# A macaron layer on one core: the first block's start, the weight counts and the last stores rearranged

## The chip, the cores and the metric

The kernel runs on one core of a Trainium2 chip. A core has a matrix engine (TensorE, PE in the profile; its weight loads are PEld), a vector engine (VectorE, DVE), an engine for activation functions (ScalarE, ACT), a general one (GpSimd, POOL) and SyncE (SP), which here only starts transfers. Each works through its own instructions in order; they meet at semaphores. Transfers between the chip's memory (DRAM) and the on-chip memory are queued by SP, ACT or POOL and carried out by 16 shared DMA engines. PE writes into eight banks of a separate accumulation memory (PSUM).

The metric is the device time of one launch in microseconds (us). Three timed runs of the kernel before gave 1446.25 in the median (1444.95 to 1446.85).

## The reference, cut to what matters

```python
x = L0_attn_x                                         # (4, 1024, 256), float32
x = x + 0.5 * ffn(layernorm(x))
x = x + s4d(layernorm(x))                             # long convolution by FFT, gelu, @ W.T + b
x = x + 0.5 * ffn(layernorm(x))                       # the same weights again

def ffn(x):                                           # D = 256, HID = 1024
    h = silu((x @ w1.T) * w1_s) * ((x @ w2.T) * w2_s)
    h = gelu((h @ h1.T) * h1_s)
    h = gelu((h @ h2.T) * h2_s)
    return (h @ w3.T) * w3_s                          # the weights hold -1, 0 and 1
```

## The kernel before

The 4096 rows are cut into eight blocks of 512. The blocks go through the first feed-forward turn (`f0` to `f7`) and, after the convolution of their batch entry, through the second (`g0` to `g7`): sixteen blocks, one after another, in the loop at L817 to L831.

**One block.** `norm` (L199) takes the mean and variance of each row on DVE (`bn_stats`, `bn_aggr`), the square root on ACT, then a reciprocal and four scalings on DVE. `transposed` (L220) turns the rows on PE into two banks `pt` and brings them back as `xt`: a copy rounded to the fast format fp32r and, by `low_part` (L216), what the rounding lost, so that two fast products stand for one exact one. `ffn` (L248) then runs layer one for m = 0 to 7 (banks `pa`, `pb`; silu on ACT, the gate product on DVE, L260, a rounded copy `ha` on ACT and its low part on DVE), layers two and three (banks `p`, gelu on ACT, copies `h`), and the output product `po` (L296), two row groups to a bank. The result is scaled on DVE (L304), the block's rows are added on POOL (L312) and SP stores it (L313). A block has 64 products 128x512 in layer one and 128 in each of the two others, and 64 products 128x256 for `po`.

**Beside it.** The generator `all_aside` makes the convolution's kernel, its spectrum, and for each batch entry the mixing `mix` (forward transform, product with the spectrum, inverse transform, output product), whose steps are called from inside the blocks: `tick` is called 15 times a block. `prepare` loads and normalises the next block ahead; `ahead` calls it. Last in `all_aside` come the weight counts (`weight_checks`, L315): the fp32r weights are exact for -1, 0 and 1, and 44 loads of 256 KB each bring the given weights again and count on DVE (L329) where the held ones differ. Two are handed out per tick. At the end the counts are summed, a product over partitions gives the flag `bad` (L838 to L842), every engine reads it, and if it is not zero the whole is computed again in plain fp32. With these inputs it is zero.

**What sets the order.** The program records instructions; a scheduler of the framework then places each engine's instructions by the readiness it expects of them. An instruction of a later block can so be placed ahead of one of an earlier block. Once placed, the order is fixed: an engine that waits holds up all that is behind it.

**The start.** SP issues, in this order: the first block's 512 KB (L170), the constants (L180, with the epsilon of the norm in a column), the scales, the second block, `k_in` (L188 and L189, the inputs of the convolution's kernel), the w3 scales, `wt` and `bias`, then blocks three and four. POOL issues w1 and w2, each in two halves by rows k (L183, L184), so that any product needs all columns' halves, then h1 and h2 in four parts each (L192) and w3 (L193).

Of the kernel before, what the change touches and what calls it, by code (L numbers as in the profile page):

```python
# [2 lines left out]

# [1 line left out]

# [12 lines left out]
P = 128  # L18
# [10 lines left out]
NA, NB = 64, 16  # L29
A0, A1 = 8, 8  # L30
JQ = J // 2
N_CHECKS = 44

EPS = 1e-5
# [14 lines left out]
C_A0, C_A1 = 0, A0  # L49
C_B = C_A1 + A1  # L50
C_RE = C_B + NB
C_IM, C_MINUS_RE, C_SGN, C_EPS, C_HALF_PI = range(C_RE + 1, C_RE + 6)
C_N = C_HALF_PI + 1
CST_WIDTH = 56

# [5 lines left out]
def shape_constants():  # L61

    p = np.arange(P)
    j = np.arange(J).reshape(2, JQ).T.reshape(-1)
    k = np.arange(P)
    pos = J * p[:, None, None] + j[None, :, None]
    angle = (2 * k[None, None, :] + 1) * pos % (4 * L) * (2.0 * np.pi / (4 * L))
    forward = np.stack([np.cos(angle), -np.sin(angle)], axis=2)  # L70

    inverse = forward.transpose(3, 1, 2, 0) * (2.0 / L)

    cst = np.zeros((P, C_N), np.float64)
    cst[:, C_A0 : C_A0 + A0] = NB * np.arange(A0)
    cst[:, C_A1 : C_A1 + A1] = NB * A0 * np.arange(A1)
    cst[:, C_B : C_B + NB] = np.arange(NB)
    real = (np.arange(P) // N2) % 2 == 0
    cst[:, C_RE] = real
    cst[:, C_IM] = ~real  # L80
    cst[:, C_MINUS_RE] = -1.0 * real
    cst[:, C_SGN] = np.where(real, 1.0, -1.0)
    cst[:, C_EPS] = EPS
    cst[:, C_HALF_PI] = HALF_PI
    return (
        np.ascontiguousarray(forward.astype(np.float32)),
        np.ascontiguousarray(inverse.astype(np.float32)),
        cst.astype(np.float32),
    )
# [3 lines left out]
def macaron_layers(  # L93
# [70 lines left out]
    def positions(t, b, j, n=2):  # L164
        return t[b].rearrange("(p j) d -> p j d", j=J)[:, j : j + n, :]

    def load_x(t, blk, name):
        b, g = divmod(blk, J // JT)
        xb = work.tile([P, JT, D], F32, tag="xb", name=name, bufs=3)
        nc.sync.dma_start(xb, positions(t, b, g * JT, JT))  # L170
        return xb

    def rows(w):
# [2 lines left out]

    weights_from = nc.gpsimd if split else nc.sync

    x_first = load_x(x, 0, "x_f0")
    nc.sync.dma_start(cst_sb[:, 0:C_N], cst)  # L180
    nc.sync.dma_start(sc_sb, scales)
    for k in range(DC):
        weights_from.dma_start(w1_sb[:, k, :], rows(w1)[:, k, :])  # L183
        weights_from.dma_start(w2_sb[:, k, :], rows(w2)[:, k, :])  # L184
    x_second = load_x(x, 1, "x_f1")
    k_in = half("k_in", 4, DD)
    k_in2 = half("k_in2", 4, DD)
    nc.sync.dma_start(k_in, kin[:, 0:4, :])  # L188
    nc.sync.dma_start(k_in2[:, 0, :], kin[:, 4, :])  # L189
    for t, src in ((h1_sb, h1), (h2_sb, h2)):  # L190
        for k in range(0, KH, 2):
            weights_from.dma_start(t[:, k : k + 2, :], rows(src)[:, k : k + 2, :])  # L192
# [3 lines left out]
    nc.sync.dma_start(bias_sb, bias.partition_broadcast(P))  # L196


    def norm(t, name):  # L199

        stats = small.tile([P, JT, 6], F32, tag="stats", name=f"stats_{name}")
        mv = small.tile([P, JT, 2], F32, tag="mv", name=f"mv_{name}")
        rstd = small.tile([P, JT], F32, tag="rstd", name=f"rstd_{name}")
        for i in range(JT):
            nc.vector.bn_stats(stats[:, i, :], t[:, i, :])
        for i in range(JT):
            nc.vector.bn_aggr(mv[:, i, :], stats[:, i, :])
        nc.scalar.activation(rstd, mv[:, :, 1], AF.Sqrt, bias=column(C_EPS))
        yield
        nc.vector.reciprocal(rstd, rstd)  # L210
        for i in range(JT):
            ts(t[:, i, :], t[:, i, :], mv[:, i, 0:1], rstd[:, i : i + 1], ALU.subtract, ALU.mult)
        yield


    def low_part(t, src):  # L216

        tt(t[:, 1, :], src, t[:, 0, :].bitcast(F32), ALU.subtract)  # L218

    def transposed(xn, name):  # L220

        xt = []
        for k in range(DC):
            pt = bank(f"pt_{name}_{k}")
            for i in range(JT):
                nc.tensor.transpose(  # L226
                    pt[:, i * P : (i + 1) * P], xn[:, i, k * P : (k + 1) * P], ident
                )
            t = ring(f"xt_{name}_{k}", parts, TB, dtype=wide)
            nc.vector.tensor_copy(t[:, 0, :], pt)  # L230
            if split:
                low_part(t, pt)
            xt.append(t)
        return xt

    def linear(ps, w, m, acts):
        n = len(acts)
# [7 lines left out]
                    stop=(k == n - 1 and part == parts - 1),  # L245
                )

    def ffn(xt, src, dst, blk, name, tick, ahead):  # L248

        ha = []
        for m in range(KH):
            pa, pb = bank(f"pa_{name}_{m}"), bank(f"pb_{name}_{m}")
            linear(pa, w1_sb, m, xt)
            linear(pb, w2_sb, m, xt)
            g = half(f"g_{name}_{m}")
            t = ring(f"ha_{name}_{m}", parts, TB, dtype=wide)
            nc.scalar.activation(g, pa, AF.Silu, scale=sc_sb[:, 0, m : m + 1])  # L259
            stt(g if split else t[:, 0, :], pb, sc_sb[:, 1, m : m + 1], g, ALU.mult, ALU.mult)  # L260
            if split:
                nc.scalar.copy(t[:, 0, :], g)  # L262
                low_part(t, g)
            ha.append(t)
        for layer, w in ((2, h1_sb), (3, h2_sb)):
            hb = []
            for m in range(KH):
                ps = bank(f"p{layer}_{name}_{m}")
                linear(ps, w, m, ha)
                t = ring(f"h{layer}_{name}_{m}", parts, TB, dtype=wide)  # L270
                g = half(f"g{layer}_{name}_{m}") if split else t[:, 0, :]
                nc.scalar.activation(g, ps, AF.Gelu, scale=sc_sb[:, layer, m : m + 1])  # L272
                if split:
                    nc.scalar.copy(t[:, 0, :], g)  # L274
                    low_part(t, g)
                hb.append(t)
                if layer == 3:
                    ahead()
                if m < KH - 1:
                    tick()  # L280
            ha = hb
        ahead(last=True)
        tick()
        b, g = divmod(blk, J // JT)
        rest = []
        for i in range(0, JT, 2):
            xr = half(f"xr_{name}_{i}", 2, D)
            nc.sync.dma_start(xr, positions(src, b, g * JT + i))
            rest.append(xr)
        for i in range(0, JT, 2):  # L290
            xr = rest[i // 2]
            ps = bank(f"po_{name}_{i}")
            for e in range(2):
                for k in range(KH):
                    for part in range(parts):
                        nc.tensor.matmul(  # L296
                            ps[:, e * D : (e + 1) * D],
                            ha[k][:, part, (i + e) * P : (i + e + 1) * P],
                            w3_sb[:, k, :],
                            start=(k == 0 and part == 0),  # L300
                            stop=(k == KH - 1 and part == parts - 1),
                        )
            y = half(f"y_{name}_{i}", 2, D)
            stt(  # L304
                y,
                ps.rearrange("p (e d) -> p e d", e=2),
                0.5,
                w3s_sb[:, None, :].to_broadcast([P, 2, D]),
                ALU.mult,
                ALU.mult,  # L310
            )
            nc.gpsimd.tensor_tensor(y, xr, y, ALU.add)  # L312
            nc.sync.dma_start(positions(dst, b, g * JT + i), y)  # L313

    def weight_checks():  # L315

# [9 lines left out]
        for n, (src, held) in enumerate(todo):  # L326
# [8 lines left out]
                ALU.not_equal,  # L335
                accum_out=miss[:, n : n + 1],
            )
            if n % 2:
                yield

# [457 lines left out]
    def all_aside():  # L800


        yield from kernel_steps()
        yield from kernel_spectrum()
        for b in range(B):
            while ("f", 2 * b + 1) not in done:
                yield
            yield from mix(b)
            done.append(("m", b))
        if split:  # L810
            yield from weight_checks()

    aside = all_aside()
    for _ in norm(x_first, "f0"):
        pass
    xt = transposed(x_first, "f0")
    for n, (turn, blk) in enumerate(blocks):  # L817
        following = []
        steps = [prepare(*b, following) for b in blocks[n + 1 : n + 2]]
# [5 lines left out]
                next(step, None)  # L825

        src, dst = (x, x1) if turn == "f" else (x2, out)
        ffn(xt, src, dst, blk, f"{turn}{blk}", lambda: next(aside, None), ahead)
        done.append((turn, blk))
        xt = following  # L830
    for _ in aside:  # L831
        pass


    if split:
        total = small.tile([P, 1], F32, name="total")
        ones = small.tile([P, 1], F32, name="ones")
        nc.vector.memset(ones, 1.0)  # L838
        nc.vector.tensor_reduce(total, miss[:, 0:N_CHECKS], axis=mybir.AxisListType.X, op=ALU.add)
        ps = psum.tile([1, 1], F32, tag="ps", name="p_bad")  # L840
        nc.tensor.matmul(ps, total, ones, start=True, stop=True)
        nc.vector.tensor_copy(bad, ps)  # L842


def macaron_kernel(tc: tile.TileContext, *args):
# [72 lines left out]
```

## Time and profile before

| What | us |
|---|---|
| median of three timed runs | 1446.25 |
| the profiled execution, its own time | 1447.1 |
| its span, first to last instruction | 1445.3 |
| TensorE matmul busy | 1418.6 |
| VectorE busy | 835.7 |
| ScalarE busy | 672.7 |
| GpSimd busy | 76.1 |
| statistics of the first block start | 4.54 |
| first product of layer one starts | 17.07 |
| layer two of the first block runs unbroken from | 40.29 |
| output product of the first block starts | 98.15 |
| last output product ends | 1437.67 |

A row of a group or timeline reads: start, duration, engine, line, operation, what it writes and from what, shapes, how many; in square brackets how long the engine stood idle before it and what ended that. A matmul's record overlaps the next one's: 128x512 products are recorded with 390 ns, but 256 of them in a row take 58.03 us, 0.227 us each. "clock" is the share of its full clock that PE was granted.

### The profile page before, as it was taken

To read this page: it belongs to the slowest core of one execution; us is meant where nothing else is said; L and a number is where in the kernel's file an instruction comes from. 1 tells how busy PE (TensorE), PEld (TensorE's weight loads), DVE (VectorE), ACT (ScalarE), POOL (GpSimd) and SP (SyncE) were. 2 spreads that over 40 slices of the span, in tenths; PEclk is the share of its full clock that TensorE was granted. 3 is DMA by queue.
4 is the path that set the end of the run, shared out by engine and by line. 5 is a ranking of instruction groups with operands and counts; after the bars stand their busy time and mean duration, and the time that the engine had idled before them with its cause. 6 is when DMAs were issued, how large, how long until landed. Compare 5 with 4: busy or idle time off the path is not lost.

```text
span 1445.3 us, 18115 instructions
## 1 busy us (share of the span) xinstructions
PE 1418.6 (98%) x7074; PEld 1199.6 (83%) x7074; DVE 835.7 (58%) x1580; ACT 672.7 (47%) x1026; POOL 76.1 (5%) x75
## 2 busy tenths in 40 slices
PE   5999999999999999999999999999999999999997
PEld 4788888888888888888888888888888888888886
DVE  5777666862745487542676622866447666564511
ACT  3677458743534454334553433534345343443432
POOL 2000000000000000020000010000010000100000
PEclk9999999999999999999999999999999999999999
DMA  9110000100122030130130130220121201633000
GB/s 363 40 37 8 15 31 0 45 1 30 44 74 73 30 102 16 44 109 8 31 106 15 55 102 1 73 73 30 44 88 44 74 30 44 219 117 103 23 8 17
DMA packets 43038, 85.50 MB, mean 59 GB/s; under 512 B 4800, under 2 KB 10048, under 8 KB 42944
## 3 DMA queue, kind: packets, MB, share of 16 engines
q1 hardware_dynamic: 39152, 72.73, 15.4%
q0 software_dynamic: 3792, 11.54, 2.3%
q8 instruction: 57, 0.93, 0.3%
q14 instruction: 37, 0.30, 0.1%
HBM read 69.05 MB, written 15.20 MB: 58 GB/s over the span
## 4 chain that ended last, share of the span: by engine, by line
PE 93%; DMA 3%; DVE 3%; ACT 1%; issue 0%; POOL 0%; SPq 0%; POOLq 0%; DVEq 0%
PE p_f L240 31%; PE p_g L240 30%; PE po_g L296 4%; PE po_f L296 4%; PE pa_g L240 4%; PE pb_g L240 4%; PE pa_f L240 4%; PE pb_f L240 4%; PE pi L737 2%; PE pf_m L567 2%; PE pw L757 2%; PE pk L498 1%; DMA x_f<-in_x_dram 1%; DMA k_in<-in_kin_dram 1%; DMA x_g<-x 1%; PE pt_f L226 1%
## 5 line engine op out<-in xcount | busy, mean ns | idle before, releaser
L240 PE MATMUL p_f<-ha_f,h_sb 128*128 128x512 f32 x1024 | 239.9, 393 | 1.8 <-ACT ha_f L262 0.9
L240 PE MATMUL p_f<-h_f,h_sb 128*128 128x512 f32 x1024 | 238.9, 392 | 0.0
L240 PE MATMUL p_g<-h_g,h_sb 128*128 128x512 f32 x1024 | 236.0, 390 | 0.0
L240 PE MATMUL p_g<-ha_g,h_sb 128*128 128x512 f32 x1024 | 235.0, 390 | 0.0
L240 PEld LDWEIGHTS p_f<-ha_f,h_sb 128*128 128x128 f32 x1024 | 192.7, 189 | 43.7 <-ACT ha_f L262 1.7
L240 PEld LDWEIGHTS p_g<-h_g,h_sb 128*128 128x128 f32 x1024 | 192.2, 188 | 39.8
L240 PEld LDWEIGHTS p_g<-ha_g,h_sb 128*128 128x128 f32 x1024 | 192.1, 188 | 39.7
L240 PEld LDWEIGHTS p_f<-h_f,h_sb 128*128 128x128 f32 x1024 | 191.5, 188 | 39.7
L272 ACT ACTIVATE g_g<-p_g,sc_sb 128x512 f32<-128x512 f32 x128 | 88.3, 690 | 273.7 <-PE p_g L240 273.6
L218 DVE TENSOR_TENSOR h_g<-g_g,h_g 128x512 fp32r<-128x512 f32 x128 | 88.5, 691 | 215.2 <-ACT h_g L274 215.2
L218 DVE TENSOR_TENSOR h_f<-g_f,h_f 128x512 fp32r<-128x512 f32 x128 | 88.2, 691 | 202.9 <-ACT h_f L274 202.6
L272 ACT ACTIVATE g_f<-p_f,sc_sb 128x512 f32<-128x512 f32 x128 | 88.0, 689 | 219.1 <-PE p_f L240 217.2
L274 ACT CAST h_g<-g_g 128x512 fp32r<-128x512 f32 x128 | 79.4, 620 | 4.0
L274 ACT CAST h_f<-g_f 128x512 fp32r<-128x512 f32 x128 | 78.9, 618 | 3.2
L259 ACT ACTIVATE g_g<-pa_g,sc_sb 128x512 f32<-128x512 f32 x64 | 43.7, 688 | 68.2 <-PE pa_g L240 64.9
L240 PE MATMUL pa_f<-xt_f,w_sb 128*128 128x512 f32 x256 | 70.3, 395 | 1.9 <-DVE xt_f L230 1.2
L240 PE MATMUL pb_f<-xt_f,w_sb 128*128 128x512 f32 x256 | 69.2, 391 | 0.0
L240 PE MATMUL pa_g<-xt_g,w_sb 128*128 128x512 f32 x256 | 68.6, 390 | 0.0
L240 PE MATMUL pb_g<-xt_g,w_sb 128*128 128x512 f32 x256 | 68.4, 389 | 0.0
L296 PE MATMUL po_g<-w_sb,h_g 128*128 128x256 f32 x512 | 65.7, 289 | 1.7 <-DVE h_g L218 1.7
L296 PEld LDWEIGHTS po_g<-w_sb,h_g 128*128 128x128 f32 x512 | 63.8, 196 | 2.5 <-DVE h_g L218 2.3
L260 DVE SCALAR_TENSOR_TENSOR g_g<-pb_g,sc_sb,g_g 128x512 f32<-128x512 f32 x64 | 47.6, 748 | 30.9 <-PE pb_g L240 25.2
(216 smaller groups left out, 1632.0 us busy)
## 6 DMA issues: line engine op xcount, KB each, us to landing
h_sb<-in_h_dram POOLq DMA_DIRECT2D x8, 1024.0 KB, 22.8
given<-in_h_dram SPq DMA_DIRECT2D x32, 256.0 KB, 5.1
kr<-k_hat SPq DMA_DIRECT2D x20, 256.0 KB, 2.6
ki<-k_hat SPq DMA_DIRECT2D x20, 256.0 KB, 2.8
x_f<-in_x_dram SPq DMA_DIRECT2D x8, 512.0 KB, 4.1
xr_f<-in_x_dram SPq DMA_DIRECT2D x16, 256.0 KB, 4.1
x<-y_f SPq DMA_DIRECT2D x16, 256.0 KB, 2.4
xm<-x SPq DMA_DIRECT2D x8, 512.0 KB, 4.5
```

The source lines that it names most:

```text
L218: tt(t[:, 1, :], src, t[:, 0, :].bitcast(F32), ALU.subtract)
L226: nc.tensor.transpose(pt[:, i * P : (i + 1) * P], xn[:, i, k * P : (k + 1) * P], ident)
L240: nc.tensor.matmul(ps, w[:, k, m * P : (m + 1) * P], acts[k][:, part, :], start=(k == 0 and part == 0), stop=(k == n - 1 and part == parts ...
L259: nc.scalar.activation(g, pa, AF.Silu, scale=sc_sb[:, 0, m : m + 1])
L260: stt(g if split else t[:, 0, :], pb, sc_sb[:, 1, m : m + 1], g, ALU.mult, ALU.mult)
L272: nc.scalar.activation(g, ps, AF.Gelu, scale=sc_sb[:, layer, m : m + 1])
L274: nc.scalar.copy(t[:, 0, :], g)
L296: nc.tensor.matmul(ps[:, e * D : (e + 1) * D], ha[k][:, part, (i + e) * P : (i + e + 1) * P], w3_sb[:, k, :], start=(k == 0 and part == 0) ...
L498: nc.tensor.matmul(pk[0:NA, at + i, :, :].rearrange("p h b -> p (h b)"), a[:, i].rearrange("p a b -> p (a b)"), qd[d1 // per_tile][:, at + ...
L567: nc.tensor.matmul(ps[e][:, part, :], m[:, e, part, :], rows_of(q + JQ * e), start=True, stop=True)
L737: nc.tensor.matmul(banks[dc][e][:, q * P : (q + 1) * P], vs[q + JQ * e][:, part, dc * P : (dc + 1) * P], m[:, e, part, :], start=(part == ...
L757: nc.tensor.matmul(ps[:, e * D : (e + 1) * D], yts[dc][j // JQ][:, (j % JQ + e) * P : (j % JQ + e + 1) * P], wt_sb[:, dc, :], start=(dc == 0),
```

## The change

It has five parts.

1. **First block ahead on VectorE.** The first block's rows are loaded in two halves, one by SP and one by ACT. Its norm is recorded in two parts. Its transposes go by row group, so that both banks fill together, and ACT makes one of the two rounded copies. `ffn` of the first block is recorded inside `tc.issue_after(last_split.ins)`, so that its instructions are placed behind the last low part of the first block's transposes. The epsilon is a small tile set on DVE, no column of the constants, and ACT takes one square root of it at once, which loads its table.
2. **Weights by columns.** w1 and w2 come as columns 0 to 255 of both, then columns 256 to 1023 of both. The second block and `k_in` go to POOL's queue, behind those four loads and ahead of h1.
3. **Identity products until rows arrive.** 14 products of the 128x128 identity with itself, into a bank that nobody reads, stand first on PE.
4. **Weight counts spread.** After the first four blocks one count is handed out on every third tick, from a generator of its own; the sum and the flag follow in it after the 44th.
5. **Last stores smaller.** In the last block the last two row groups have a bank each; each is scaled and added on DVE and stored by itself (128 KB), where before both were scaled together, added on POOL and stored as 256 KB.

```diff
@@ loads
-    x_first = load_x(x, 0, "x_f0")
+    x_first = work.tile([P, JT, D], F32, tag="xb", name="x_f0", bufs=3)
+    for i, queue in ((0, nc.sync), (2, nc.scalar)):
+        queue.dma_start(x_first[:, i : i + 2, :], positions(x, 0, i))
+    eps = small.tile([P, 1], F32, name="eps", bufs=1)
+    nc.vector.memset(eps, EPS)
+    unused = small.tile([P, 1], F32, name="unused", bufs=1)
+    nc.scalar.activation(unused, eps, AF.Sqrt)
...
-    for k in range(DC):
-        weights_from.dma_start(w1_sb[:, k, :], rows(w1)[:, k, :])
-        weights_from.dma_start(w2_sb[:, k, :], rows(w2)[:, k, :])
-    x_second = load_x(x, 1, "x_f1")
+    for cols in (slice(0, 256), slice(256, HID)):
+        weights_from.dma_start(w1_sb[:, :, cols], rows(w1)[:, :, cols])
+        weights_from.dma_start(w2_sb[:, :, cols], rows(w2)[:, :, cols])
+    x_second = load_x(x, 1, "x_f1", queue=weights_from)
...
-    nc.sync.dma_start(k_in, kin[:, 0:4, :])
-    nc.sync.dma_start(k_in2[:, 0, :], kin[:, 4, :])
+    weights_from.dma_start(k_in, kin[:, 0:4, :])
+    weights_from.dma_start(k_in2[:, 0, :], kin[:, 4, :])
@@ transposed
+        for k, i in sorted(order, key=lambda o: o[1]) if first else order:
+            nc.tensor.transpose(
+                pts[k][:, i * P : (i + 1) * P], xn[:, i, k * P : (k + 1) * P], ident
+            )
+        xt = [ring(f"xt_{name}_{k}", parts, TB, dtype=wide) for k in range(DC)]
+        if first:
+            last = nc.vector.tensor_copy(xt[0][:, 0, :], pts[0])
+            nc.scalar.copy(xt[1][:, 0, :], pts[1])
...
+            if split:
+                last = low_part(xt[k], pts[k])
+        return (xt, last) if first else xt
@@ ffn, the output
-            nc.gpsimd.tensor_tensor(y, xr, y, ALU.add)
-            nc.sync.dma_start(positions(dst, b, g * JT + i), y)
+            add_on.tensor_tensor(y, xr, y, ALU.add)
+            nc.sync.dma_start(positions(dst, b, g * JT + i, n), y)
+            if final and i + 2 == JT:
+                for e in range(2):
+                    ps = bank(f"po_{name}_{i + e}")
+                    result(ps, i + e, 1)
+                    finish(ps[:, 0:D], y[:, e : e + 1, :], rest[i // 2][:, e : e + 1, :],
+                           i + e, 1, nc.vector)
+            else:
+                ps = bank(f"po_{name}_{i}")
+                result(ps, i, 2)
+                finish(ps, y, rest[i // 2], i, 2, nc.gpsimd)
@@ weight_checks
-            if n % 2:
-                yield
+            yield
+        total = small.tile([P, 1], F32, name="total")
...
+        nc.vector.tensor_copy(bad, ps)
@@ the loop
+    def tick():
+        nonlocal ticks
+        next(aside, None)
+        ticks += 1
+        if ticks > 4 * STEPS and ticks % 3 == 0:
+            next(checks, None)
+    warm = bank("warm")
+    for i in range(N_WARM):
+        nc.tensor.matmul(warm[:, 0:P], ident, ident, start=(i == 0), stop=(i == N_WARM - 1))
-    for _ in norm(x_first, "f0"):
+    for _ in norm(x_first, "f0", parts_of=2):
         pass
-    xt = transposed(x_first, "f0")
+    xt, last_split = transposed(x_first, "f0", first=True)
...
-        ffn(xt, src, dst, blk, f"{turn}{blk}", lambda: next(aside, None), ahead)
+        with tc.issue_after(last_split.ins) if n == 0 else nullcontext():
+            ffn(xt, src, dst, blk, f"{turn}{blk}", tick, ahead, n + 1 == len(blocks))
```

`STEPS` is 15, `N_WARM` 14. The weights, the products and their number are the same, save the 14 of part 3.

## The prediction

> **What bounds the kernel now.** I read the page first, then busy time by stage, then the timeline of the first 45 us and of the end, and last the one block where TensorE waits in between. Times in us are from the start of the profiled execution.
>
> ```profile
> PE 1418.6 (98%) x7074; PEld 1199.6 (83%) x7074; DVE 835.7 (58%) x1580; ACT 672.7 (47%) x1026; POOL 76.1 (5%) x75
> ...
> PEclk9999999999999999999999999999999999999999
> ...
> PE 93%; DMA 3%; DVE 3%; ACT 1%; issue 0%; POOL 0%; SPq 0%; POOLq 0%; DVEq 0%
> ```
>
> TensorE (PE) is the bound and 93% of the chain that ended last. What can be saved lies where it does not run. The busy time by stage shows where:
>
> ```profile
> core 0: us, PE busy (x) PEld busy (x) DVE busy (x) ACT busy (x) POOL busy (x), PEclk, DMA share, GB/s
> 0.00:17.07 17.07, 2.26 (x9) 1.48 (x9) 6.66 (x28) 3.16 (x4) 8.62 (x18) 1.00 0.93 307
> 17.07:40.29 23.22, 20.65 (x77) 15.00 (x77) 16.87 (x42) 13.16 (x21) 0.88 (x1) 1.00 1.13 400
> 40.29:106.06 65.77, 65.77 (x317) 55.70 (x318) 47.18 (x106) 46.95 (x61) 1.60 (x1) 0.97 0.05 17
> 106.06:1268.43 1162.37, 1160.55 (x5849) 983.60 (x5847) 695.15 (x1273) 544.18 (x842) 57.25 (x49) 1.00 0.16 52
> 1437.67:1445.30 7.63, 0.10 (x2) 0.00 (x0) 0.74 (x2) 0.00 (x0) 1.26 (x1) 0.68 0.18 56
> ```
>
> Three places: the head (no product before 17.07, then 77 records in 23.2 us), a little before 1268.43, and 7.63 us after the last product. The head in order of time:
>
> ```profile
> 10.82 1.08 DVE L205 BATCH_NORM_STATS2 stats_f<-x_f 128x6 f32<-128x256 f32 x3 [4.60 <-DMA x_f<-in_x_dram]
> ...
> 12.90 0.34 DVE L414 TENSOR_SCALAR k_in<-k_in,cst_sb 128x128 f32<-128x128 f32 x1 [0.92 <-DMA k_in<-in_kin_dram]
> 13.10 1.38 DVE L212 TENSOR_SCALAR x_f<-x_f,mv_f,rstd_f 128x256 f32<-128x256 f32 x4
> ...
> 17.07 1.72 PE L240 MATMUL pa_f<-xt_f,w_sb 128*128 128x512 f32 x2 [1.20 <-DVE xt_f L230]
> ...
> 23.95 1.41 DVE L205 BATCH_NORM_STATS2 stats_f<-x_f 128x6 f32<-128x256 f32 x4 [4.50 <-DMA x_f<-in_x_dram]
> ...
> 26.50 1.40 DVE L205 BATCH_NORM_STATS2 stats_f<-x_f 128x6 f32<-128x256 f32 x4 [0.86 <-DMA x_f<-in_x_dram]
> ...
> 28.10 2.03 DVE L260 SCALAR_TENSOR_TENSOR g_f<-pb_f,sc_sb,g_f 128x512 f32<-128x512 f32 x3
> ```
>
> VectorE (DVE) works in order. The first block's scaling (13.10) stands behind the second block's statistics and behind `k_in`, though its own data was there at 4.54. Later the first gate product (28.10) stands behind the statistics of blocks three and four. So layer two runs without a break only from 40.29, where the chain of waits has 244 of its 256 products left; they end at 97.5.
>
> **The head, step by step.** *Until the first product.* The rows come in two halves on two queues, the same 512 KB, so I keep 4.4 for their landing. Then, on DVE without anything between: 4 statistics at 0.33 apart, 4 aggregates at 0.09, 2 reciprocals at 0.16, 4 scalings at 0.33 make 3.3; ScalarE's (ACT) square roots lie beside it, their table now loaded before; some 0.4 for handing over. Last scaling at 8.1, last transposes 8.6, copy 0.68: the first product could start at about 9.5 instead of 17.07. The constant moved to a memset and the dummy square root cost nothing: DVE and ACT are idle until 4.5.
>
> *The weights.* The built order of the changed program puts on PE, after pa and pb of m=0 and m=1 (four products), pa and pb of m=2. Those need columns 256 to 1023 of w1 and of w2, and PE does not pass by a waiting product. So the real start is W, the landing of the last of the four weight loads; the early columns save only five products. W comes from bytes:
>
> ```profile
> GB/s 0 62 372 141 251 337 354 364 361 392 397 386 388 395 382 397 400 397 409 411 408 408 422 419 422 430 419 411 430 408 422 419 401 393 378 122 5 15 0 0
> ```
>
> These are 40 slices of 1.125 us of the first 45 us; summed: 1.31 MB by 6.75, 2.52 by 10.1, 3.41 by 12.4, 4.28 by 14.6, 9.28 by 27.0. In the run before, GpSimd's (POOL) queue waits show the four loads landed at about 7.5, 10.4, 12.5 and 14.1, with 1.07, 1.61, 2.66 and 3.44 MB at or ahead of them: 1.5 to 2.8 after the sum reached it, 2.0 in the mean. In the changed program rows (0.52), small constants (0.04) and weights (2.10) go with what SyncE (SP) issues meanwhile: w3 scales, wt, bias (0.52), the third block (0.52), and, from 8.7 when the first buffer is free, the fourth (0.52). That is 3.97 to 4.23 MB: reached at 13.8 to 14.5, plus 2.0. **W = 16.2**; the ends are 13.3 (no SP load ahead: 3.2 MB, plus 1.5) and 17.3.
>
> Here a rule stands against the row. The Trainium skill (DMA: Bandwidth & Descriptors, "Anatomy of one DMA") prices a load at 2.0 us plus bytes over 436 GB/s; with 2.6 MB of rows and weights that would be some 8 us after issue at 1.3, W near 9.5, and a gain of 15. The trace has 14.1 for the same 2.1 MB of weights, because other queues share the engines; I take the row.
>
> *From W.* PE has 59 of layer one's 64 products left. The first ones before ran at 0.43 apart until 20.4 (3.4 us), then 0.227 (58.03/256). Will the 14 identity products change this? 128x128 fp32 products of this form take 0.11 (pi: 7.14/64) at full clock, twice that when slow: 3 us, from 2.5 to 5.5, before ten idle microseconds. The skill (TensorE: Matmul & The Clock Gate, Part 1) says that some 3.4 us of work opens the clock and an idle window of the same length closes it. By that they buy nothing, and by the trace's 3.4 us row they are too short as well; if they held, 8 x 0.2 = 1.6 would come off. I take nothing. Layer one: 8 x 0.43 + 51 x 0.227 = 15.0, if ACT and DVE keep up. They have 1.3 and 1.27 each per m against PE's 1.82, but DVE now waits for block two and `k_in`, which moved behind the weights on POOL's queue: 0.78 MB more, W+2.1. From there the order gives the first gate at W+4.1; ACT then carries two table loads (1.28 each) and a root, gates 2 to 4 at W+9.5 to W+10.7, the last low part at W+17.5. PE needs that one at W+18.2. So it just fits, by 0.7, and PE flows from layer one into two. The h1 weights (9.3 MB, 27.0 plus 2.0 = 29) come before W+17 = 33.
>
> End of layer three: W + 15.0 + 58.0 = 89.2 against 97.5. **Gain 8.3** (11.2 and 7.2 at the ends of W; the slow clock of 40 to 45, which cost 1.7, goes with the gap). Later blocks follow 8.3 earlier.
>
> **The weight counts.** Before, 44 loads and counts came in one stretch:
>
> ```profile
> 1268.43 6.79 PE L296 MATMUL po_g<-w_sb,h_g 128*128 128x256 f32 x42 [1.31 <-DVE h_g L218]
> ...
> 1270.00:1275.00 5.00, 5.00 (x32) 5.00 (x32) 2.08 (x6) 0.00 (x0) 1.28 (x1) 0.68 0.13 49
> ```
>
> DVE was full from 1250 to 1270, h7's low part came late, PE lost 1.31 + 0.41, and then ran at clock 0.68 for 5 us (1.6): 3.3 in all. Spread out, each count is 0.69 + 0.08 of DVE, five per block, 3.9 in some 81 to 102 us of a block where DVE is at most 78% busy: hidden. Each also adds a load to SP and holds a buffer; in the order a buffer comes free 4 to 20 DVE instructions (2.4 to 12 us) before the count, while a load takes 0.33 + 2.4 to 5.1. Some counts will hold DVE for 1 to 2 us. ACT's results wait on DVE then, but PE uses them a layer later, save at layer ends. SP's stores queue behind such a load too; their readers come a block later. Bounds: nothing, and 0.3 for each of 9 blocks; I take 0.5. **Gain 2.8.** The final sum and flag product (0.2) move inside; nothing.
>
> **The last stores.**
>
> ```profile
> 1437.69 0.69 DVE L304 SCALAR_TENSOR_TENSOR y_g<-po_g,w3s_sb 128x512 f32<-128x512 f32 x1 [2.78 <-PE po_g L296]
> 1438.52 1.26 POOL L312 TENSOR_TENSOR y_g<-xr_g,y_g 128x512 f32<-128x512 f32 x1 [2.18 <-DVE bad L842]
> ```
>
> From the last product to the store's issue: 0.69, then the flag's 0.13, POOL 1.26: 2.1. After: two DVE operations on 256 columns, 0.42 each (the 256-wide scaling has 0.41), 0.06 between: 0.9. The landing (3.3) and the 2.2 behind it stay; half the bytes may save 0.3 more, and PE's branch at the end (4.1 from 1439.1) starts earlier too. **Gain 1.2.**
>
> **The sum.** 8.3 + 2.8 + 1.2 = 12.3: span 1445.3 to 1433.0, profiled execution 1447.1 to 1434.8. The median of the timed runs is 0.85 under that one: 1446.25 - 12.3 = **1434.0 us**. A change of 0.2% (2.9 us) is about what can be told from none.
>
> **Rivals.**
> *The weights come sooner, or the clock stays open* (0.15). For it: only the SP loads stand between 13.3 and 16.2. Against it: they are issued by 5 us. W = 13.3 and the clock open: 11.2 + 1.6 + 2.8 + 1.2 = 16.8, 1429.5.
> *The first block still stands behind DVE* (0.17). For it: the margin is 0.7, and DVE again waits for block two first. If `k_in` lands 4 us later or ACT's table loads fall worse, layer two starts 4 later and the slow clock (1.7) returns: gain 6.6, 1439.6.
> *The counts cost more than they free* (0.05): slower. Mechanism: a count waits for its load on DVE just before a block's last low part, and PE stalls as it did at 1268 for 3.3. Head and tail and the freed stall give 12.8; four of nine blocks with it eat that, all nine give 1446.25 - 12.8 + 29.7 = 1463. Against it: in the trace some forty loads of k_hat factors reach DVE in the same way, and no wait for them is among its 25 longest.
> *The order is not what is said* (0.01): the built order shows the first block's DVE work unbroken, so hardly; 1446.
>
> **How the numbers follow.** 0.62 for 1434.0, with 1431 to 1437 of its own; the rest as above. The range reaches over most of the two neighbours: 1429.5 to 1439. Faster 0.93, same 0.02, slower 0.05.
>
> **What would show it.** First product at 9 to 10, four or five products, then a wait ended by w_sb until about 16; layer two unbroken from about 31, layer three's end near 89; no wait of PE for h_g of over 0.5 at a block's end; store issued 0.9 to 1.0 after the last product. Wrong would be a wait for ha_f in layer two over 2 us, or waits for counts that PE feels.

## The result and the profile after

The changed kernel took 1436.53 us in the median (1435.89 to 1437.07, four runs), the one before beside it 1445.62 (1444.95 to 1446.85, four runs): a ratio of 0.9936, 95% interval 0.9919 to 0.9953. That is 9.1 us less; the prediction had 12.3 less, 1434.0. The profiled execution has a span of 1435.2 against 1445.3, 10.1 less.

The page of the changed kernel, its busy row and its chain by engine:

```profile
PE 1420.1 (99%) x7102; PEld 1203.3 (84%) x7102; DVE 834.3 (58%) x1584; ACT 674.2 (47%) x1030; POOL 79.1 (6%) x77
...
PE 97%; DVE 1%; DMA 1%; POOL 0%; issue 0%; POOLq 0%
```

PE rose from 93% of the chain to 97%: what is left is almost all matrix work. Where the rest sits is in the busy time by stage (columns as in the prediction: PE, its weight loads, DVE, ACT, POOL, then clock, transfer share, GB/s):

```profile
10.45:16.75 6.30, 1.69 (x5) 0.86 (x5) 1.27 (x2) 1.25 (x1) 1.20 (x2) 0.91 1.09 413
16.75:22.60 5.85, 5.82 (x14) 4.66 (x15) 2.94 (x11) 1.42 (x3) 3.77 (x5) 0.52 1.13 424
22.60:33.08 10.48, 10.48 (x48) 8.65 (x47) 9.56 (x21) 9.32 (x15) 0.00 (x0) 1.00 1.13 419
33.08:91.10 58.02, 58.02 (x258) 47.99 (x258) 42.98 (x109) 45.03 (x61) 0.00 (x0) 1.00 0.14 45
1428.28:1435.20 6.92, 0.00 (x0) 0.00 (x0) 0.85 (x2) 0.00 (x0) 0.00 (x0) 0.78 0.19 64
```

Five products run before 16.75, then PE is full but at clock 0.52, then full at 1.00. Layers two and three take 58.02 without a break and end at 91.10. The timeline of PE shows what the first stretch waits for:

```profile
2.58 6.33 PE L880 MATMUL warm<-ident 128*128 128x128 f32 x28 [2.58 <-POOL ident masks.py:199]
8.72 1.06 PE L248 MATMUL pt_f<-ident,x_f 128*128 128x128 f32 x8
10.45 0.50 PE L267 MATMUL pa_f<-xt_f,w_sb 128*128 128x512 f32 x1 [0.67 <-DVE xt_f L254]
...
13.43 0.50 PE L267 MATMUL pa_f<-xt_f,w_sb 128*128 128x512 f32 x1 [1.79 <-DMA w_sb<-in_w_dram]
16.78 0.77 PE L267 MATMUL pb_f<-xt_f,w_sb 128*128 128x512 f32 x1 [2.85 <-DMA w_sb<-in_w_dram]
```

The 14 identity products fill PE until 8.9; the last scaling of the rows was done at 7.5:

```profile
6.66 0.84 DVE L227 TENSOR_SCALAR x_f<-x_f,mv_f,rstd_f 128x256 f32<-128x256 f32 x2
```

Four products follow, then the fifth and sixth, pa and pb of m=2, each wait for the late columns of w1 and w2. The first gain, up to the end of layer three, is 97.5 - 91.1 = 6.4. The output products of the next four blocks keep this lead of 6.4, so the head accounts for all of it up to where the counts begin. The last product ends at 1428.28 instead of 1437.67, 9.39 earlier, so the counts brought 3.0. The end:

```profile
1427.49 2.54 SPq L341 DMA_DIRECT2D out_dram<-y_g  x2
1427.74 0.52 PE L323 MATMUL po_g<-w_sb,h_g 128*128 128x256 f32 x3
...
1428.30 0.42 DVE L332 SCALAR_TENSOR_TENSOR y_g<-po_g,w3s_sb 128x256 f32<-128x256 f32 x1 [0.97 <-PE po_g L323]
1428.76 0.42 DVE L340 TENSOR_TENSOR y_g<-xr_g,y_g 128x256 f32<-128x256 f32 x1
```

Scaling and addition take 0.9 as priced, to 1429.18. SP's two stores are one group here; the first was issued for 2.07 us, so the last went out only at 1429.6. From the last product to the end are 6.92 against 7.63: 0.7.

### The profile page after: what moved, and what is told of

Read it like the earlier page. It is cut to its first block, busy times and chain, and to the rows that moved or that the text cites. A ratio compares the mean times of both kernels' runs of the same rounds, so it can differ in the third digit from the quotient of the medians.

```text
span 1435.2 us, 18151 instructions
## 1 busy us (share of the span) xinstructions
PE 1420.1 (99%) x7102; PEld 1203.3 (84%) x7102; DVE 834.3 (58%) x1584; ACT 674.2 (47%) x1030; POOL 79.1 (6%) x77
## 4 chain that ended last, share of the span: by engine, by line
PE 97%; DVE 1%; DMA 1%; POOL 0%; issue 0%; POOLq 0%
PE p_g L267 32%; PE p_f L267 31%; PE po_g L323 4%; PE po_f L323 4%; PE pb_f L267 4%; PE pa_f L267 4%; PE pa_g L267 4%; PE pb_g L267 4%; PE pi L791 2%; PE pw L811 2%; PE pf_m L621 2%; PE pk L552 1%; DMA w_sb<-in_w_dram 1%; PE pf_k L621 0%; PE pt_g L248 0%; PE pt_f L248 0%
## 5 line engine op out<-in xcount | busy, mean ns | idle before, releaser
L267 PE MATMUL p_f<-ha_f,h_sb 128*128 128x512 f32 x1024 | 237.0, 391 | 0.0
L286 ACT ACTIVATE g_f<-pa_f,sc_sb 128x512 f32<-128x512 f32 x64 | 43.3, 688 | 44.8 <-PE pa_f L267 43.9
L323 PE MATMUL po_f<-w_sb,h_f 128*128 128x256 f32 x512 | 64.0, 285 | 0.2 <-DVE h_f L240 0.2
```

The costliest lines, as they stand in the source:

```text
L267: nc.tensor.matmul(ps, w[:, k, m * P : (m + 1) * P], acts[k][:, part, :], start=(k == 0 and part == 0), stop=(k == n - 1 and part == parts ...
L323: nc.tensor.matmul(ps[:, e * D : (e + 1) * D], ha[k][:, part, (i + e) * P : (i + e + 1) * P], w3_sb[:, k, :], start=(k == 0 and part == 0) ...
```

## The experiments

"Output from" is the start of the first block's output product in the profiled execution, the best single mark of the head. It is one execution: the changed kernel and counts_end have the same head in the program and lie 1.25 apart. The kernel before was timed beside each; its median was 1444.94 to 1446.37 in the five sessions, so the ratio is the fairer comparison, and medians of different sessions that differ by under about 1 us are not told apart.

| Kernel | Output from | Median (range), us | Ratio to before, 95% |
|---|---|---|---|
| before | 98.15 | 1445.62 (1444.95 to 1446.85) | 1 |
| order_only | 95.92 | 1443.59 (1441.61 to 1445.86) | 0.9983 (0.9976 to 0.9990) |
| the changed kernel | 91.74 | 1436.53 (1435.89 to 1437.07) | 0.9936 (0.9919 to 0.9953) |
| identity_12 | 91.36 | 1436.16 (1436.05 to 1436.41) | 0.9932 (0.9915 to 0.9949) |
| counts_end | 90.49 | 1437.57 (1436.99 to 1439.31) | 0.9944 (0.9924 to 0.9963) |
| identity_11 | 89.78 | 1432.99 (1432.21 to 1434.27) | 0.9908 (0.9891 to 0.9924) |
| halves | 89.43 | 1434.64 (1433.55 to 1435.63) | 0.9929 (0.9913 to 0.9946) |
| rows | 88.36 | 1432.38 (1431.72 to 1433.35) | 0.9904 (0.9884 to 0.9924) |
| no_identity | 85.75 | 1430.23 (1429.99 to 1430.52) | 0.9888 (0.9870 to 0.9907) |
| no_id_tail | 85.59 | 1431.39 (1431.31 to 1431.78) | 0.9900 (0.9880 to 0.9920) |
| no_id_rows | 84.89 | 1429.88 (1429.63 to 1430.68) | 0.9890 (0.9870 to 0.9910) |
| no_id_loads_late | 84.08 | 1433.44 (1433.18 to 1434.50) | 0.9915 (0.9899 to 0.9932) |
| no_id_late_store | 84.03 | 1433.06 (1432.74 to 1433.31) | 0.9910 (0.9893 to 0.9926) |
| loads_late | 83.74 | 1431.42 (1430.37 to 1433.28) | 0.9901 (0.9880 to 0.9921) |

### Part 1 alone (order_only)

The kernel before with the first block's order, the split rows and the early table load; against the changed kernel, these edits and those of counts_end and no_id_tail below:

```diff
-N_WARM = 14
+N_WARM = 0
...
-    for cols in (slice(0, 256), slice(256, HID)):
-        weights_from.dma_start(w1_sb[:, :, cols], rows(w1)[:, :, cols])
-        weights_from.dma_start(w2_sb[:, :, cols], rows(w2)[:, :, cols])
+    for k in range(DC):
+        weights_from.dma_start(w1_sb[:, k, :], rows(w1)[:, k, :])
+        weights_from.dma_start(w2_sb[:, k, :], rows(w2)[:, k, :])
-    x_second = load_x(x, 1, "x_f1", queue=weights_from)
-    weights_from.dma_start(k_in, kin[:, 0:4, :])
-    weights_from.dma_start(k_in2[:, 0, :], kin[:, 4, :])
+    x_second = load_x(x, 1, "x_f1")
+    nc.sync.dma_start(k_in, kin[:, 0:4, :])
+    nc.sync.dma_start(k_in2[:, 0, :], kin[:, 4, :])
```

> Part 1 alone, on the kernel before: the first block's rows, norm and transposes ahead on VectorE and its feed-forward behind them; loads, counts and stores as before. If the order on VectorE was what gained at the head, layer two of the first block runs unbroken from about 34 and the span is about 1439 (6.4 less than 1445.3). If the queues decide, VectorE still waits for the third and fourth block's rows (landing near 24 and 27 as before) before its first gate product, TensorE runs out of banks meanwhile, layer two starts near 40 and the span is 1443 to 1446.

It is 2.5 us faster than the 1446.08 measured beside it, although the first product starts at 9.50 instead of 17.07. In PE's timeline, then in DVE's:

```profile
28.15 2.07 PE L267 MATMUL pa_f<-xt_f,w_sb 128*128 128x512 f32 x4 [6.65 <-DVE g_f L287]
```

```profile
24.16 1.41 DVE L217 BATCH_NORM_STATS2 stats_f<-x_f 128x6 f32<-128x256 f32 x4 [9.18 <-DMA x_f<-in_x_dram]
...
27.36 2.05 DVE L287 SCALAR_TENSOR_TENSOR g_f<-pb_f,sc_sb,g_f 128x512 f32<-128x512 f32 x3
```

PE stops for 6.65 because the first gate product stands on DVE behind the statistics of the third block, whose rows DVE waited 9.18 for. The 7.6 us that the early start wins go into a wait for rows one step later. That is the second of the two expectations (span 1443.8). no_id_rows below has the same weights by rows and no identity products either, but the second block and `k_in` on POOL's queue, the spread counts and the small stores: there this wait is gone, and it is 13.7 faster. Counts and stores bring 2.2 to 4.5 of that (below), so some 9 to 11.5 come with the queue and the order that follows from it. The queue was not moved alone.

### The identity products (no_identity, identity_11, identity_12)

```diff
-N_WARM = 14
+N_WARM = 0     # no_identity; 11 and 12 in the two others
```

> The changed kernel without the 14 identity products. If the landing of the last weight load decides (16.75 in the changed kernel), with the clock closed again by then, the products at 10.4 run slow, but layer two still starts near 33 and the span stays within 0.5 of 1435.2. If the identity products carry their clock into layer one, the span grows by 1 to 2.

It came out 6.3 us faster than the changed kernel, with intervals that don't meet: neither the prediction nor the two expectations of this run said so. PE's timeline:

```profile
9.36 0.80 PE L267 MATMUL pa_f<-xt_f,w_sb 128*128 128x512 f32 x1 [0.57 <-DVE xt_f L254]
...
16.82 1.19 PE L267 MATMUL pb_f<-xt_f,w_sb 128*128 128x512 f32 x4 [0.66 <-DMA w_sb<-in_w_dram]
...
26.93 3.34 PE L267 MATMUL p_f<-ha_f,h_sb 128*128 128x512 f32 x14
```

The late columns of w2 land when they did, at 16.8, but pb of m=2 now waits 0.66, not 2.85. The scheduler places by the readiness that it expects. With no identity products it placed all of m=0 and m=1 ahead, and then pa of m=2, whose columns had landed meanwhile: 20 products beside the landing. With 14 of them ahead on PE it put m=2 fifth and sixth. The busy time of no_identity up to the landing and from there to layer two:

```profile
9.36:16.82 7.46, 6.81 (x20) 4.99 (x20) 1.26 (x2) 3.33 (x5) 1.45 (x3) 1.00 1.09 407
16.82:26.93 10.11, 10.11 (x44) 8.37 (x45) 8.13 (x15) 6.09 (x12) 3.76 (x5) 1.00 1.13 421
```

This divides the difference at the end of layer one, 33.08 against 27.09. At the landing the changed kernel has 5 products done and no_identity 20; 15 at 0.227 are 3.4. From the landing on, the changed kernel takes 16.3 for its 59 products, 2.9 more than at 0.227 each, because the clock has closed in the wait; no_identity takes 10.3 for its 44, up to 27.09, 0.3 more, with its slow products already done ahead of the landing. So 3.4 is work not done during the wait, and 2.6 is the clock.

Two runs show the place by itself, with one identity product between them:

> The changed kernel with 12 identity products instead of 14. The built order still puts pa and pb of m=2 as fifth and sixth product, so PE stands on w2's late columns with four products done. Theory 'placement' (the identity products cost by where the builder puts m=2): as the changed kernel, layer two from 32 to 34, median 1435 to 1437. Rival 'their own time' (each of the fourteen takes 0.44 us of PE before the transposes): 0.9 us less, 1435.6.

> One identity product fewer than identity_12. In the built order pa of m=2 is still fifth, but pb of m=2 comes after the 17 other products of m=0 and m=1. Theory 'placement': PE waits for w1's late columns (landed near 13.5) with four products done, then has some 19 products of m=0 to m=2 to run beside the landing of w2's late columns (16.8), so layer two starts 4 to 6 us earlier than in identity_12: from 27 to 29.5, median 1430 to 1432.5. Rival 'their own time': 0.4 us less than identity_12. Rival 'the clock' (the identity products matter by the granted clock): no difference between 11 and 12.

With 12, pa and pb of m=2 are both early; with 11 pb of m=2 comes after m=0 and m=1. PE's timelines, of 12 and then of 11:

```profile
13.08 0.49 PE L267 MATMUL pa_f<-xt_f,w_sb 128*128 128x512 f32 x1 [2.08 <-DMA w_sb<-in_w_dram]
16.40 0.77 PE L267 MATMUL pb_f<-xt_f,w_sb 128*128 128x512 f32 x1 [2.83 <-DMA w_sb<-in_w_dram]
```

```profile
14.53 2.07 PE L267 MATMUL pa_f<-xt_f,w_sb 128*128 128x512 f32 x4 [3.86 <-DMA w_sb<-in_w_dram]
```

From 14 to 12 the median falls by only 0.4, and the first block's output comes 0.4 earlier, where two products take 0.9 of PE. With 11 the second wait is gone. The median is 3.2 us lower, where one identity product takes 0.45, and the ranges don't touch (the first block's output is 1.6 earlier in the profiled executions, that of 11 being the longest of its four runs). It fell short of the 1430 to 1432.5 expected: w1's late columns came at 14.5, not 13.5, and the wait for them remains. So the place of one product explains a quarter to a half of the 6.3. The rest may lie in the wait for pa of m=2 and the clock that closes in it, in the transposes (at 8.72 behind the identity products, 6.59 without them) and in DVE's order: without identity products the gates of the first block are placed ahead of the second block's remaining statistics, with them behind. No run separates these.

### By rows or by columns (rows, no_id_rows, halves), and SP's loads (loads_late)

```diff
-    for cols in (slice(0, 256), slice(256, HID)):
+    for cols in (slice(0, 512), slice(512, HID)):
```

That is halves. rows and no_id_rows have the loop over k that the first diff shows, no_id_rows also `N_WARM = 0`.

> The changed kernel, with w1 and w2 loaded by rows (k = 0, then 1) as before instead of by columns; identity products kept. In the built order seven products on k = 0 come first, and the second product on k = 1 of the pb's needs the last of the four loads, so PE stands until about 16.8 either way. Theory 'the columns buy almost nothing beside the identity products' (the prediction's five products): within 1.5 us of the changed kernel, layer two from 31.5 to 34, median 1435 to 1437.5. Rival (columns are a main part of the gain): layer two from 36 or later, median over 1439.

> As rows, but without identity products. Built order: nine products on k = 0, then seven on k = 1 of the pa's, then pb of m=0 on k = 1, which needs the last load (16.8): 16 products done by then against 22 with columns. Theory (the columns pay only once the identity products are gone): 6 x 0.227 and a later opening of the clock, 1.4 to 3 us slower than the 1430.2 without identity products and with columns: 1431.6 to 1433.2. Rival (columns buy nothing at all): 1430 to 1430.5.

> The changed kernel, identity products kept, with each weight split at column 512 instead of 256: four loads of 512 KB in 2 KB pieces, the first two of which hold m = 0 to 3 whole. The seven products that the built order puts first, and the 25 after them, then need the first two loads alone. Theory (the identity products cost because the order they bring reaches columns that land last): PE has 32 products of work from about 10.5 on, the late halves land at 13 to 16.5 behind it, no wait for weights of over 0.5 us after the first product, layer two from 25.5 to 28 with small waits for ScalarE as by rows; median 1430 to 1433. Size of the pieces: if 2 KB pieces keep up with the 4 KB pieces of rows, the fourth load lands at 14 to 14.5; if pieces smaller than 4 KB lose their share to SyncE's loads, at 15.5 to 16.8. Rival (the identity products cost by their own time on PE, whatever the split): as the changed kernel, 1435.5 to 1437.

The theory missed for rows and no_id_rows, on the good side. By rows the changed kernel is about 4 us faster, and without identity products rows and columns are equal (1429.88 and 1430.23), as that run's rival said within 0.1. (By rows a product on k = 0 needs only the first half of its own weight, not all four loads.) POOL's queue shows when the weights landed: it issues a part of h1 each time that a weight load has landed, and the issue after the fourth is, in the changed kernel, by rows, by halves, and with SP's loads late:

```profile
16.94 0.71 POOL L201 DMA_DIRECT2D h_sb<-in_h_dram  x1 [2.54 <-DMA w_sb<-in_w_dram]
```

```profile
14.35 0.70 POOL L201 DMA_DIRECT2D h_sb<-in_h_dram  x1 [0.94 <-DMA w_sb<-in_w_dram]
```

```profile
16.95 0.72 POOL L201 DMA_DIRECT2D h_sb<-in_h_dram  x1 [1.40 <-DMA w_sb<-in_w_dram]
```

```profile
11.60 0.72 POOL L201 DMA_DIRECT2D h_sb<-in_h_dram  x1 [1.22 <-DMA w_sb<-in_w_dram]
```

The same 2.1 MB, 2.6 us apart. By rows a partition's contiguous piece is 4 KB, by halves 2 KB, by columns 1 and 3 KB. The page's part on queues, for the window from 5 to 9 us, in the changed kernel and then by rows (q0 is POOL's, q1 SP's; packets, MB, share of the 16 engines):

```profile
q1 hardware_dynamic: 525, 0.59, 57.1%
q0 software_dynamic: 378, 0.52, 45.6%
```

```profile
q0 software_dynamic: 219, 0.79, 57.7%
q1 hardware_dynamic: 324, 0.23, 25.7%
```

And by halves:

```profile
q0 software_dynamic: 384, 0.74, 60.7%
q1 hardware_dynamic: 467, 0.47, 43.8%
```

By rows the weights moved 0.79 MB in those 4 us and SP's loads 0.23; by columns 0.52 and 0.59. In packets the queues' shares hardly differ: POOL's has 0.7 to 0.8 for each of SP's in all three, while a packet of POOL's holds 1.4 KB by columns, 1.9 by halves and 3.6 by rows. That fits a rule of the Trainium skill (DMA: Bandwidth & Descriptors, "Queues, rings and completion order"): a DMA engine goes round-robin between its queues "at *packet* granularity". But the page's packet typically holds several pieces and the trace's here about one, and the runs show shares and landings, not the turns. This window alone does not settle the landing either: by halves 0.74 MB moved in it, nearly as by rows, and the last load still landed as late as by columns. Halves and columns cut the two weights into 1024 pieces each, rows into 512. A smaller rival stands: by rows POOL was through issuing the four loads 0.7 us sooner. So that rows land 2.6 earlier is shown, and that the pieces are the reason is argued.

In the profiled execution of rows the identity products also took only 4.74, and the first product came at 9.06. PE then waited 1.6 for weights, so the early start is not what rows gained by.

loads_late takes the other side of the contest away:

```diff
-    nc.sync.dma_start(w3s_sb, w3_s.partition_broadcast(P))
-    nc.sync.dma_start(wt_sb, rows(wt))
-    nc.sync.dma_start(bias_sb, bias.partition_broadcast(P))
+    weights_from.dma_start(w3s_sb, w3_s.partition_broadcast(P))
+    weights_from.dma_start(wt_sb, rows(wt))
+    weights_from.dma_start(bias_sb, bias.partition_broadcast(P))
...
-            xb = x_second if blk == 1 else load_x(x, blk, f"x_{name}")
+            xb = x_second if blk == 1 else load_x(
+                x, blk, f"x_{name}", queue=weights_from if blk < 4 else nc.sync
+            )
```

> The changed kernel with the w3 scales, wt, bias and the third and fourth blocks taken from SP's queue and put behind w3 on GpSimd's. If the landing of the last weight load decides, 2.66 MB stand ahead of it, not 4.2: it lands near 13, layer two starts near 29 if the clock is slow for 5.8 us again and near 27 if it stays open, and the span is 1429 to 1431.5. If VectorE or ScalarE decide, layer two starts near 32 to 33 and the span is 1434 to 1435.5.

By columns still, the fourth load lands 5.3 us earlier (11.60, where 13 was expected), no wait for weights shows among PE's waits, and the median is 5.1 lower. Not all of that need be the weights: the second block's rows, which DVE waits for, also come 4.5 earlier. halves tests the place in PE's order from the other side: it keeps the identity products and lets the first two loads hold all that the early products need. PE waited for weights 0.3 us, as expected, but the median of 1434.64 missed its 1430 to 1433 and lies between the theory and the rival. PE's waits in halves, and DVE's first statistics of the second block and first gates:

```profile
PE pa_f L267 <- DVE g_f L287: 1.4, 1, 1.4
PE pa_f L267 <- ACT g_f L286: 1.2, 1, 1.2
```

```profile
17.93 1.08 DVE L217 BATCH_NORM_STATS2 stats_f<-x_f 128x6 f32<-128x256 f32 x3 [6.26 <-DMA x_f<-in_x_dram]
...
21.02 1.39 DVE L287 SCALAR_TENSOR_TENSOR g_f<-pb_f,sc_sb,g_f 128x512 f32<-128x512 f32 x2
```

Now DVE and ACT hold PE: DVE stands 6.26 for the second block's rows, until 17.9, before it makes the first gates at 21.0. That is the prediction's second rival; in the changed kernel it is hidden behind the wait for weights.

### Both cures together, and the store (no_id_loads_late, no_id_late_store)

The edits of no_identity and loads_late together; the second with this besides:

```diff
-            nc.sync.dma_start(positions(dst, b, g * JT + i, n), y)
+            out_on.dma_start(positions(dst, b, g * JT + i, n), y)
...
                         nc.vector,
+                        nc.scalar if e == 0 else nc.sync,
```

> The changed kernel without identity products and with w3 scales, wt, bias and the rows of blocks three and four put behind w3 on GpSimd's queue. Without identity products the first product was at about 9.4 and layer two from 27.1; with the loads late and identity products layer two started at 24.9 with no wait for weights. Together: weights are not waited for, the clock has to open in layer one (8 products at 0.43), layer two from 24.5 to 26.5, but the waits in block 0's output (1 to 2 us together) stay. Median 1429 to 1431.5. If the two gains added up fully it would be 1425; they don't, since both remove the same wait for w2's late columns.

> As no_id_loads_late, with the first of the two last half stores issued by ScalarE's queue instead of SyncE's. In the changed kernel's profile SyncE spent 2.07 us on one issue at the end, and the last half store was issued only after it. Theory: with the other half elsewhere SyncE issues the last half at once, 0.05 to 0.1 after the last addition, and the time from the last product to the end goes from 6.9 to 6.3 to 6.6: median 0.3 to 0.6 below no_id_loads_late. Rival (the end is set by the landing and PE's closing branch alone): no difference.

The first missed its 1429 to 1431.5. At 1433.44 it is slower than no_identity, and by its median than loads_late (whose slowest run, 1433.28, reaches its range). Layer two runs from 25.26 and the output product stands at 84.08, 1.7 ahead of no_identity; PE's waits show what follows:

```profile
PE pa_f L267 <- DVE xt_f L258: 1.2, 1, 1.2
PE po_f L323 <- ACT h_f L301: 1.0, 1, 1.0
```

The last copies of the first block are behind ACT's and DVE's work for the convolution's kernel, and the next block's turned rows are late too. And then the clock closes:

```profile
91.00:97.00 6.00, 6.00 (x38) 5.85 (x37) 4.41 (x8) 0.00 (x0) 1.27 (x1) 0.73 0.00 0
```

6 us at a mean of 0.73 are 1.6 more. The second block's output starts 3.0 behind that of no_identity (178.68 against 175.72), and it stays so; the waits and the clock explain 3.8 of this swing of 4.6. loads_late has the wait for h_f too, 0.9, but in its profiled execution the clock stayed open.

With the middle store on ACT's queue the median is 0.4 lower, which lies in the theory's 0.3 to 0.6, but the ranges overlap and the spans are 1431.4 and 1431.3: in both profiles SP issued the last store 0.04 after the addition, so there was no long issue to take away, and the theory was not tested. The 2.07 us of the changed kernel is a thing of some executions: the longest issue at the end took 0.49 to 2.07 in those with three stores on SP.

### The counts and the last store (counts_end, no_id_tail)

```diff
-            yield
+            if n % 2:
+                yield
...
+        yield from checks
...
-        if ticks > 4 * STEPS and ticks % 3 == 0:
-            next(checks, None)
```

That is counts_end, two counts per tick after the last mixing. no_id_tail has no identity products and the old last store:

```diff
-            if final and i + 2 == JT:
+            if False:
```

> The changed kernel with the weight counts again two per tick after the last mixing. If the crowd on VectorE cost the stall of the block g5, it returns: TensorE waits near 1258 for h_g, then a slow clock, and the span is 1437.5 to 1438.5. If the spread counts cost as much as they freed, 1435.

> The changed kernel without identity products, and with the last store as before: one addition of 512 columns on GpSimd and one store of 256 KB. Without identity products 6.5 us lay between the last product and the end; in the kernel before it was 7.6. Theory (the prediction's 1.2): 1.0 to 1.3 more than the 1430.2, so 1431.2 to 1431.6, and 7.5 to 7.7 us behind the last product. Rival (the end is set by PE's closing branch or by the landing, and 0.7 as in the changed kernel's profile is all): 0.5 to 0.8 more.

With the counts at the end, PE's wait is back:

```profile
PE po_g L323 <- DVE h_g L240: 1.6, 2, 1.3
```

The span of that execution, 1435.1, is the rival's number by luck: its head happened to be 1.25 ahead of the changed kernel's (output from 90.49), and the last product ends at 1428.74, 0.46 behind it. So bunched counts cost 1.7 in this execution; the medians differ by 1.0. The clock stayed at 1.00 over the stall this time; the kernel before lost some 1.6 more to it. So spreading brings 1.0 to 3.3.

The old store costs 1.2 in the median (1431.39 against 1430.23). In the profiles the stretch behind the last product is 7.5 against 6.5, as priced.

## Why the prediction was right, and where it was not

**The bound and the direction.** PE as the bound and the three places held: 9.1 (timed) or 10.1 (span) for 12.3, inside the range. In the span 2.2 were missing: 1.9 at the head and 0.5 at the store, less 0.2 that the counts brought more.

**"The first product could start at about 9.5."** It started at 10.45; without identity products at 9.36. They were priced at 3 us, from 2.5 to 5.5. An fp32 product of this form leaves two records (28 for 14), each 0.226 here, so 6.33: long enough to open the clock, but they ended at 8.9, behind the last scaling. The row that they were priced from, pi, was read as one record for one product; its 64 records are 32 products.

**"W = 16.2."** Measured 16.75, off by 0.55. Its reason, that SP's loads stand between 13.3 and 16.2, is shown by loads_late and was even too small: without them 11.6. What was missing is that cutting the weights by columns moves W: by rows it was 14.35, near the 14.1 of the kernel before.

**"By that they buy nothing ... I take nothing."** This is the step that failed. The clock did open (the first four products are 0.23 to 0.34 apart) and did close again, as said. But the products cost 6.3: the prediction took the built order, m=2 as fifth and sixth, as given, and did not ask what had put it there. The number did not suffer, since the sum rested on that order and so carried the cost already; what was wrong is what part 3 of the change does. "The early columns save only five products" was true of that order and a consequence of the identity products.

**"Layer one: 15.0."** From 16.75 to 33.08 are 16.3. The term too small is the slow stretch: 8 products at 0.43 were taken from the kernel before, whose slow start lasted 3.4; here 14 came in 5.85. PE did flow into layer two without a wait, and ACT and DVE kept up by the small margin given. So the end of layer three was 91.1, not 89.2: 0.55 from W, 1.3 from the clock.

**"Gain 2.8" for the counts.** 3.0. The 0.5 for counts that wait shows as the output products of the later blocks slipping from 6.4 to 5.9 us ahead of the old ones (the chain reaches that of block g4 at 1163.61 for 1169.48); the stall before 1268 is gone.

**"Gain 1.2" for the store.** 0.7 in the profiled execution, where SP's long issue held the last store back by 0.4; 1.2 between no_identity and no_id_tail.

**The rivals.** "The weights come sooner" and "the first block still stands behind DVE" did not come for this kernel, but each is what loads_late and halves showed. No count was felt by PE.

The best version found is the changed kernel without identity products, with the weights by columns or by rows: 1430.23 and 1429.88, which can't be told apart, 6 us under the change as it was.

## What to carry to other kernels

A filler at the head of an in-order engine is also an input to the scheduler: compare the built order with and without it, not only its own time. Products that waited for weights were helped here by loading them by rows, in 4 KB pieces, and by keeping another queue's loads out of their way; both can be read from the landing times. When one wait goes, run the combined version before adding gains: here two cures of 5 to 6 us gave less together than either.

## What the hardware showed beyond expectation

**The clock closes for 3.4 or 6.8 us, on a fixed grid.** In the changed kernel it fell to 0.50 at 15.6 and was back at 22.4, as two windows of its profile show (the clock is the third number from the end; 0.79 is 0.42 us at half clock):

```profile
15.00:16.00 1.00, 0.00 (x0) 0.00 (x0) 0.00 (x0) 0.00 (x0) 0.00 (x0) 0.79 1.04 412
22.00:23.00 1.00, 1.00 (x5) 0.80 (x4) 0.06 (x1) 0.98 (x2) 0.35 (x1) 0.79 1.11 418
```

It was closed from 15.1 to 22.0 with 12 identity products, 13.2 to 20.0 with 11, 13.0 to 19.8 in counts_end and 24.3 to 31.1 in order_only, 6.8 each. But in the kernel before it closed for only 3.4, at 40.98 and again at 1269.77, and so it did in no_id_loads_late at 90.81. Windows of 0.25 us place the falls to some 0.01: the two of the kernel before are 1228.79 apart, 360 times 3.4133, and the two of order_only, at 24.27 and 1266.72, are 364 times 3.4133 apart. So within an execution these changes lie on multiples of one period, and the closed stretches are one or two periods long. In the changed kernel, with 12, with 11 and in counts_end, PE worked 0.8 to 2.2 us of the first period after the fall, and the clock stayed closed for a second; in order_only PE worked 2.95 of the second, and it opened.

What a wait costs therefore hangs on where in the grid it falls: in counts_end the clock fell so early that the slow stretch ended 2.6 sooner. The skill (TensorE: Matmul & The Clock Gate, Part 1) has a free-running window of 3.4 us, and for one kernel 6, 11 or 14 slow products at its start, by where in the window it starts. The grid here agrees with such a window.

**Slow at a granted clock of 1.00.** In no_identity the products from 9.36 to 13 run at 0.43 each while the record says 1.00. In these traces the record shows a clock that has closed again, not the start before it first opened.

**Store issues on SP.** With three stores at the end most issues take 0.33 to 0.39, but in seven of ten profiles one of the three took 1.20 to 2.07. The reason is not shown.
